# A fused four-layer network on one core: the scan layer's dt projected tile by tile, its output projection and its state sums moved in the engines' order

## The chip, the cores and the metric

The kernel runs on one core of a Trainium2 chip. A core has five engines with queues of their own: TensorE (PE, with its weight loads shown apart as PEld), VectorE (DVE), ScalarE (ACT), GpSimd (POOL) and SyncE (SP, which here only issues DMAs). Each works through its own queue in order, and they wait for each other through semaphores. The metric is device time in microseconds, the median of the runs. The kernel before takes 3452.4 us (three runs, 3451.87 to 3458.52). The profile is one more execution of the same program.

## The reference

Four residual layers follow each other, each on the group-normalised image `x` of shape (3, 256, 48, 48): an attention block, a 3x3 convolution whose kernel is mixed from 8 experts, a plain 3x3 convolution, and a selective scan (Mamba). The change is in the scan layer alone. Cut to what matters it computes, for each image, over 2304 tokens in order:

```python
xn = layernorm(x) * norm_w + norm_b              # 256 channels per token
x_in, z = split(in_proj(xn))                     # 512 each
u = silu(causal_conv4(x_in) + conv_b)
dt_raw, B, C = split(x_proj(u))                  # 16, 16, 16
dt = softplus(dt_proj(dt_raw) + dt_proj_b)       # 512
h = h * exp(dt * A) + dt * B * u                 # 512 x 16 states, per token
y = (sum over states of h * C + u * D) * silu(z)
out = out_proj(y)                                # 256, added to x
```

## The kernel before

The first three layers end at about 2020 us of the span; the rest is the scan layer. Tokens go in chunks of 384 (`CH`), 18 chunks in all, 6 for each image. The 512 inner channels are 4 tiles of 128 (`m`). For the scan itself 32 channels times 4 states lie on the 128 partitions, so a tile needs 16 scans of 384 tokens.

A chunk is 8 **steps** (`m`, `h`): four tiles in two halves of 8 scans each. One scan (`scan`, L1766, on DVE) reads a decay `exp(dt * A)` from one of three slots `ps_da`, which ACT fills (`decay`, L1758): decay number n + 3 is issued behind scan n, so ACT works three scans ahead and no more. The driving term `dt * u * B` is filled into `hs` half by DVE (`fill_upper`, L1719, from PSUM) and half by POOL (L1733). After a step POOL multiplies the states by C (`times_c`, L1783), and a step later PE sums them over the states into `ps_y` (`add_states`, L1795 and L1800). `spread_pe` (L1689) spreads half of the dt * u rows over the partitions for DVE's fill, `spread` (L1681) does the other half and dt itself by DMA from DRAM, where `keep_dt` has put them (L1335, L1337). `gate` (L1807, DVE) multiplies the sum by silu(z), three steps behind.

All other work of the layer is laid between the scans by hand. A step has two **half-steps** of four scans, so a chunk has 16, numbered j = 0 to 15. Each has places at which stages are issued: MID (behind the second scan and its decay), DONE (behind the third), LATE (behind the fourth) and PE_ (in even half-steps behind LATE; in odd ones at the end of the step, behind `fill` and `times_c`, and ahead of `add_states` and `spread_pe`). Three lists say which stage goes where, and for which chunk: `plan` prepares the next chunk (+1) and the norm of the one after (+2), `after` finishes z and writes the output of the previous chunk (-1), `gating` projects z. `keep_order` ties PE, DVE, ACT and POOL to the written order within the scans. SP's queue is not tied: the planner that builds the program places the DMAs by its own costs, so their order is seen only in the trace. The conv layers ahead of the scans, among whose products `early_preparation` lays the first chunk's stages, are ordered by the planner too.

Two PSUM banks (`bank[0]`, `bank[1]`, shown as ps_g) serve all these stages, so a stage's matmul waits until the copy of the stage before has emptied its bank. The stages which the change touches, by line: `group_scale` L1213, `less_mean` L1222, `square_mean` L1229, `centre` L1235 and L1237, `inverse_root` L1241 and L1242, `normalise` L1246, `taps` (conv and u projection) L1264, `take_u` L1273, `silu` L1278 with the return to the exp and ln tables at L228, `project_u` L1284, `take_dbc` L1292, `project_dt` L1310, `softplus` L1319 to L1321, `take_dt` L1326 and L1327, `keep_dt` L1331, `project_z` L1341, `take_z` L1349, `project_y` L1353 and L1355, `store` L1365.

## Time and profile before

| | us |
|---|---|
| median of three runs | 3452.4 |
| the profiled execution | 3452.73 |
| its span, first to last instruction | 3451.2 |
| first scan starts | 2025.81 |
| last scan starts | 3428.7 |
| one chunk in the middle (2721.98 to 2800.41) | 78.43 |
| POOL busy in it | 76.33 |
| DVE busy in it | 75.43 |
| PE busy in it | 66.34 |
| ACT busy in it | 61.62 |

A line of the timeline gives the start, the length in us, the engine, the line of the kernel, the operation with its output and inputs, and how many of a kind were merged; in brackets stands how long the engine had been idle before, and what ended that. In a view of waits, a line names who waited for whom, the total in us, how often, and the longest. In a view of stretches, busy times by engine are followed by the clock granted to PE, the DMA share and GB/s. The names `x`, `u`, `wconv` stand for big buffers that the scan layer reuses: for instance `ps_g L1310 out of wconv` is the projection of dt. The scan period repeats with a chunk; the chunk whose half-step 0 starts at 2734.23 is the one most often looked at.

### The profile page before, as it was taken

What the parts mean: (1) busy time and instruction counts of PE and PEld (TensorE: products, weight loads), DVE (VectorE), ACT (ScalarE), POOL (GpSimd) and SP (SyncE); (2) the same over time, 40 slices, a digit from 0 to 9 for tenths busy, and PEclk for the clock granted to TensorE, in tenths of its full rate; (3) what the DMA queues carried; (4) which work ended last, traced back from release to release, by engine and by line L of the source; (5) the groups of instructions that cost most, each with busy time, mean ns of one, the idle gap of its engine ahead of it and who ended that gap; (6) DMA issues with size and microseconds to landing.
All of it is one profiled execution on the core that took longest, in us unless ns stands there. A gap on an engine that the chain in (4) does not pass through costs nothing. (4 is left out here: it accounts for less than half of the span.)

```text
span 3451.2 us, 51999 instructions
## 1 busy us (share of the span) xinstructions
PE 3115.5 (90%) x20170; PEld 1496.8 (43%) x20170; DVE 2937.4 (85%) x3306; ACT 2353.3 (68%) x3508; POOL 1430.3 (41%) x385
## 2 busy tenths in 40 slices
PE   7999999999999999879999988888888888888885
PEld 4334343443433335457677753333344443333331
DVE  4799899859899994589965379999999999999998
ACT  3788888748888884422224467777777777777774
POOL 0000000000000001110000059999999999999997
PEclk9999999999999999999999998889999999988987
DMA  4000000010000003756302134444544444544441
GB/s 178 14 8 10 8 10 8 8 42 5 11 6 8 10 8 112 240 190 222 133 22 67 46 97 115 109 105 114 120 102 115 102 109 113 119 114 107 116 111 43
DMA packets 167603, 273.95 MB, mean 79 GB/s; under 512 B 30049, under 2 KB 134561, under 8 KB 165426
## 3 DMA queue, kind: packets, MB, share of 16 engines
q1 hardware_dynamic: 154114, 250.48, 26.9%
q10 hardware_dynamic: 13232, 20.06, 1.8%
q8 instruction: 160, 2.62, 0.3%
q14 instruction: 97, 0.79, 0.1%
HBM read 223.12 MB, written 47.10 MB: 78 GB/s over the span
## 5 line engine op out<-in xcount | busy, mean ns | idle before, releaser
L641 ACT ACTIVATE pt<-ps_s 128x1024 f32<-128x1024 f32 x972 | 942.4, 1022 | 154.7 <-PE ps_s L637 142.1
L1766 DVE TENSOR_TENSOR_SCAN hs<-ps_da,hs 128x385 f32<-128x385 f32 x1152 | 1003.9, 937 | 30.7 <-ACT ps_da L1758 27.3
L856 DVE TENSOR_TENSOR part<-part,pt 128x2048 f32<-128x2048 f32 x396 | 906.7, 2290 | 41.2 <-ACT pt L641 18.4
L1758 ACT ACTIVATE ps_da<-dtr,u 128x384 f32<-128x384 f32 x1152 | 656.5, 583 | 244.1 <-DVE hs L1766 225.9
L163 POOL TENSOR_TENSOR rstd<-ve,mhalf 128x2 f32<-128x2 f32 (+1 forms) x26 | 16.4, 631 | 1475.9 <-DVE ve L161 1475.9
L637 PE MATMUL ps_s<-q,kt 32*128 32x512 f32 (+1 forms) x4320 | 576.4, 592 | 0.1
L650 PE MATMUL acc<-pt,vt 128*32 128x512 f32 (+1 forms) x4320 | 520.9, 561 | 0.2
L1783 POOL TENSOR_TENSOR hc<-hs,x 128x3072 f32<-128x3072 f32 x72 | 445.6, 6188 | 18.9 <-DVE hs L1766 16.0
L1513 PE MATMUL ps_c<-vt,u 128*128 128x288 f32 x1728 | 432.7, 411 | 20.5 <-DVE u L262 20.5
L1783 POOL TENSOR_TENSOR hc<-hs,bc 128x3072 f32<-128x3072 f32 x71 | 437.8, 6166 | 17.3 <-DVE hs L1766 15.1
L1264 PE MATMUL ps_g<-u 128*128 128x384 f32 x1152 | 388.6, 492 | 7.4 <-ACT sz L1349 3.2
L1513 PEld LDWEIGHTS ps_c<-vt,u 128*128 128x128 f32 x1728 | 330.7, 192 | 117.1 <-issue 18.8
L1264 PEld LDWEIGHTS ps_g<-u 128*128 128x128 f32 x1152 | 214.8, 190 | 180.3 <-ACT ps_da L1758 19.3
L637 PEld LDWEIGHTS ps_s<-q,kt 32*128 32x128 f32 x4320 | 195.2, 183 | 199.1 <-issue 120.2
L1800 PE MATMUL ps_y<-hc,u 128*32 128x384 f32 x2304 | 245.0, 548 | 19.6 <-POOL hc L1783 19.1
L1733 POOL TENSOR_TENSOR hs<-dtur,x 128x1536 f32<-128x1536 f32 x72 | 248.9, 3457 | 6.3 <-DMA dtur<-dtud 6.3
L1733 POOL TENSOR_TENSOR hs<-dtur,bc 128x1536 f32<-128x1536 f32 x72 | 248.5, 3451 | 0.0
L650 PEld LDWEIGHTS acc<-pt,vt 128*32 128x32 f32 x4320 | 94.4, 108 | 353.4 <-issue 326.7
L1310 PE MATMUL ps_g<-wconv,u 17*128 17x384 f32 x144 | 79.2, 684 | 85.0 <-ACT x L1331 85.0
L1800 PEld LDWEIGHTS ps_y<-hc,u 128*32 128x32 f32 x2304 | 64.2, 117 | 177.8 <-issue 143.1
L1222 PE MATMUL ps_g<-wconv,u 128*128 128x384 f32 x144 | 80.3, 725 | 62.1 <-ACT x L1331 62.1
L321 POOL MEMSET xpad<- 128x212 f32 x12 | 5.7, 472 | 313.4 <-ACT xpad L1564 234.9
(246 smaller groups left out, 3624.0 us busy)
## 6 DMA issues: line engine op xcount, KB each, us to landing
wconv<-in_we SPq DMA_DIRECT2D x144, 384.0 KB, 4.2
dtr<-dtd SPq DMA_DIRECT2D x288, 192.0 KB, 3.9
dtur<-dtud SPq DMA_DIRECT2D x288, 96.0 KB, 4.2
wconv<-xd SPq DMA_DIRECT2D x36, 384.0 KB, 4.3
x<-bcd SPq DMA_DIRECT2D x72, 192.0 KB, 6.0
dtd<-x SPq DMA_DIRECT2D x36, 384.0 KB, 3.1
bc<-bcd SPq DMA_DIRECT2D x72, 192.0 KB, 6.0
yc<-ycat ACTq DMA_DIRECT2D x18, 576.0 KB, 4.7
```

Of the source, the lines that this page charges most:

```text
L637: nc.tensor.matmul(s[:, j, cols], kt[r, mt * P : (mt + 1) * P], q[r, :n], start=True, stop=True,)
L641: nc.scalar.activation(p[:, h0 : h0 + 2, :], s, AF.Exp)
L650: nc.tensor.matmul(acc[h * HD : (h + 1) * HD, :n], vt[:, mt, g * P + h * HD : g * P + (h + 1) * HD], p[:, h, cols], start=mt == 0, stop=mt ...
L856: ): nc.vector.tensor_tensor(part, first, p, ALU.add)
L1222: nc.tensor.matmul(bank[to], w3v["less"][:, int(to != ct), :], k.xg[:, ct, :], start=ct == 0, stop=ct == CT - 1,)
L1264: nc.tensor.matmul(bank[m % 2], w3v["wtap"][:, tap, ct, m * P : (m + 1) * P], k.xn[:, ct, tap : tap + CH], start=tap == 0 and ct == 0, sto ...
L1513: nc.tensor.matmul(pc[:, :HN], u[:, i, dy, ct, m * P : (m + 1) * P], vt[:, i, ct, dy * TW : dy * TW + HN], start=ct == 0 and dy == 0, stop ...
L1733: nc.gpsimd.tensor_tensor(states(s)[:, :, 2:4, 1:], chunks[at].rows[m][1].unsqueeze(1).broadcast_to([P, 2, 2, CH]), b_rows(s, 0, 2), ALU.mult,
L1758: nc.scalar.activation(slots[n % 3][:, 1 : CH + 1], chunks[at].rows[m][0][:, q, :], AF.Exp, scale=amat[:, col : col + 1],)
L1766: nc.vector.tensor_tensor_scan(b, slots[(8 * s + part) % 3][:, : CH + 1], b, 0.0, ALU.mult, ALU.add)
L1783: nc.gpsimd.tensor_tensor(hc, tiles[s][:, :, :, 1:], cb.broadcast_to([P, 2, 4, CH]), ALU.mult)
L1800: nc.tensor.matmul(k.y_ps[32 * q : 32 * q + 32, :CH], fold, hc[:, g, q, :], start=False, stop=h == 1 and g == 1,)
```

## The change

Everything is in the scan layer.

- dt goes tile by tile (m = 0 to 3) instead of in two pairs, through bank 0: `project_dt`, `softplus`, `take_dt` and `keep_dt` each work on one tile and have places of their own from half-step 8 to 14. Softplus has three operations of 384 columns per tile; before, Abs was done per tile, and Exp and Ln once for the 768 columns of a pair. `keep_dt` writes its two DRAM tensors per tile, 8 DMAs per chunk instead of 4, and `spread` reads from these.
- There is a new place BEGIN, behind the first scan and decay of a half-step.
- The output projection of the previous chunk goes through bank 1 in both halves. The first is issued in half-step 6 (before: 5) and stored in 8 (6), so it stands ahead of the product of u with the x projection (`project_u`, half-step 7); the second is issued at BEGIN of 9, behind the projection of the first dt tile (before: 6, ahead of `project_u`), and stored in 10 (8).
- At the end of a step, `add_states` and `spread_pe` are issued ahead of the stages of PE_ and no longer behind them. Among these stages are, in half-step 1, 3 and 7, the product of u's tile 1 (`taps`), of tile 2, and `project_u`; in 13 and 15 the squared mean and z.
- The norm of the chunk after next is centred in two pieces through bank 1 into a tile of its own, `xc`; the squares go into `xg`, and `normalise` reads `xc`. Its stages are moved by up to one half-step, as is the first of z.
- The tile `dtur` loses its 16 padding columns.

```diff
--- before.py
+++ after.py
@@ -1135,7 +1135,7 @@
         rooms["xn"] = [w3v["xn0"], w3v["xn1"]]
         pieces = [wst.tile([P, 3 * 256], F32, name="wconv") for _ in range(6)]
         halves = [t.rearrange("p (t n) -> p t n", t=2) for t in pieces]
-        for name, got in zip(("xg", "sq", "ot"), (halves[:2], halves[2:3], halves[3:5])):
+        for name, got in zip(("xg", "xc", "ot"), (halves[:2], halves[2:3], halves[3:5])):
             rooms[name] = got
         rooms["dbc"] = [halves[5][:96, j, :] for j in range(2)]
 
@@ -1215,26 +1215,27 @@
                 bias=sh[:, ct : ct + 1], scale=sc[:, ct : ct + 1],
             )
 
-    def less_mean(k):
-
-        for to in range(CT):
-            for ct in range(CT):
-                nc.tensor.matmul(
-                    bank[to], w3v["less"][:, int(to != ct), :], k.xg[:, ct, :],
-                    start=ct == 0, stop=ct == CT - 1,
-                )
+    def less_mean(k, to, at=1):
+
+        for ct in range(CT):
+            nc.tensor.matmul(
+                bank[at], w3v["less"][:, int(to != ct), :], k.xg[:, ct, :],
+                start=ct == 0, stop=ct == CT - 1,
+            )
+
+    def centre(k, to, at=1):
+        if to == 0:
+            k.xc = room(k, "xc")
+        nc.scalar.copy(k.xc[:, to, :], bank[at])
+
+    def squares(k):
+        nc.scalar.activation(k.xg, k.xc, AF.Square)
 
     def square_mean(k):
         for ct in range(CT):
             nc.tensor.matmul(
-                bank[1], mean2, k.sq[:, ct, :], start=ct == 0, stop=ct == CT - 1
+                bank[1], mean2, k.xg[:, ct, :], start=ct == 0, stop=ct == CT - 1
             )
-
-    def centre(k):
-        for ct in range(CT):
-            nc.scalar.copy(k.xg[:, ct, :], bank[ct])
-        k.sq = room(k, "sq")
-        nc.scalar.activation(k.sq, k.xg, AF.Square)
 
     def inverse_root(k):
         var = bank[1]
@@ -1243,7 +1244,7 @@
 
     def normalise(k):
         rs = bank[1].unsqueeze(1).broadcast_to([P, CT, CH])
-        nc.vector.tensor_tensor(k.xg, k.xg, rs, ALU.mult)
+        nc.vector.tensor_tensor(k.xg, k.xc, rs, ALU.mult)
 
     def tokens(k):
 
@@ -1304,37 +1305,32 @@
         k.dt = room(k, "dt")
         k.dtu = room(k, "dtu")
 
-    def project_dt(k, m0):
-        for j in range(2):
-            m = m0 + j
-            nc.tensor.matmul(
-                bank[j], w3v["dtsb"][:, m * P : (m + 1) * P], k.dbc[: DTR + 1, :],
-                start=True, stop=True,
-            )
-
-    def softplus(k, m0):
-
-        both = k.dt[:, m0 : m0 + 2, :]
-        for j in range(2):
-            nc.scalar.activation(k.dt[:, m0 + j, :], bank[j], AF.Abs)
-        nc.scalar.activation(both, both, AF.Exp, scale=-1.0)
-        nc.scalar.activation(both, both, AF.Ln, bias=1.0)
-
-    def take_dt(k, m0):
-        for j in range(2):
-            m, pdt = m0 + j, bank[j]
-            nc.vector.scalar_tensor_tensor(pdt, pdt, 0.0, k.dt[:, m, :], ALU.max, ALU.add)
-            nc.vector.tensor_tensor(k.dtu[:, m, :], pdt, k.u[:, m, :], ALU.mult)
-
-    def keep_dt(k, m0):
-        for j in range(2):
-            nc.scalar.copy(k.dt[:, m0 + j, :], bank[j])
-        if m0 == 0:
+    def project_dt(k, m, at=0):
+        nc.tensor.matmul(
+            bank[at], w3v["dtsb"][:, m * P : (m + 1) * P], k.dbc[: DTR + 1, :],
+            start=True, stop=True,
+        )
+
+    def softplus(k, m, at=0):
+
+        t = k.dt[:, m, :]
+        nc.scalar.activation(t, bank[at], AF.Abs)
+        nc.scalar.activation(t, t, AF.Exp, scale=-1.0)
+        nc.scalar.activation(t, t, AF.Ln, bias=1.0)
+
+    def take_dt(k, m, at=0):
+        p = bank[at]
+        nc.vector.scalar_tensor_tensor(p, p, 0.0, k.dt[:, m, :], ALU.max, ALU.add)
+        nc.vector.tensor_tensor(k.dtu[:, m, :], p, k.u[:, m, :], ALU.mult)
+
+    def keep_dt(k, m, at=0):
+        nc.scalar.copy(k.dt[:, m, :], bank[at])
+        if m == 0:
             k.dtd, k.dtud = {}, {}
-        d = k.dtd[m0] = dram.tile([P, 2, CH], F32, name=f"dtd{m0}")
-        nc.sync.dma_start(d, k.dt[:, m0 : m0 + 2, :])
-        d = k.dtud[m0] = dram.tile([P // 2, 2, CH], F32, name=f"dtud{m0}")
-        nc.sync.dma_start(d, k.dtu[P // 2 :, m0 : m0 + 2, :])
+        d = k.dtd[m] = dram.tile([P, CH], F32, name=f"dtd{m}")
+        nc.sync.dma_start(d, k.dt[:, m, :])
+        d = k.dtud[m] = dram.tile([P // 2, CH], F32, name=f"dtud{m}")
+        nc.sync.dma_start(d, k.dtu[P // 2 :, m, :])
 
     def project_z(k, m, j):
         for ct in range(CT):
@@ -1348,12 +1344,12 @@
             k.sz = room(k, "sz")
         nc.scalar.copy(k.sz[:, m, :], bank[j])
 
-    def project_y(k, mo, lo=0, hi=DI):
+    def project_y(k, mo, lo=0, hi=DI, at=1):
         if lo == 0:
-            nc.tensor.matmul(bank[mo], ident, k.ot[:, mo, :], start=True, stop=False)
+            nc.tensor.matmul(bank[at], ident, k.ot[:, mo, :], start=True, stop=False)
         for m in range(lo, hi):
             nc.tensor.matmul(
-                bank[mo], w("out", m * 256 + mo * P, P), k.sz[:, m, :],
+                bank[at], w("out", m * 256 + mo * P, P), k.sz[:, m, :],
                 start=False, stop=m == DI - 1,
             )
 
@@ -1361,21 +1357,24 @@
         k.ot = room(k, "ot")
         nc.sync.dma_start(k.ot, xd[k.b][:, :, k.c * CH : (k.c + 1) * CH])
 
-    def store(k, mo):
-        nc.scalar.copy(k.ot[:, mo, :], bank[mo])
+    def store(k, mo, at=1):
+        nc.scalar.copy(k.ot[:, mo, :], bank[at])
         nc.sync.dma_start(
             out[k.b, mo * P : (mo + 1) * P, k.c * CH : (k.c + 1) * CH], k.ot[:, mo, :]
         )
 
 
 
-    MID, DONE, LATE, PE_ = range(4)
+    BEGIN, MID, DONE, LATE, PE_ = range(5)
     plan = [
-        (12, MID, 2, group_scale),
-        (12, PE_, 2, less_mean),
-        (13, LATE, 2, centre),
+        (11, BEGIN, 2, group_scale),
+        (11, PE_, 2, lambda k: less_mean(k, 0)),
+        (12, MID, 2, lambda k: centre(k, 0)),
+        (12, PE_, 2, lambda k: less_mean(k, 1)),
+        (13, DONE, 2, lambda k: centre(k, 1)),
+        (13, LATE, 2, squares),
         (13, PE_, 2, square_mean),
-        (14, MID, 2, inverse_root),
+        (14, DONE, 2, inverse_root),
         (15, MID, 2, normalise),
         (15, LATE, 2, tokens),
         (0, PE_, 1, lambda k: taps(k, 0, 0, 4)),
@@ -1390,13 +1389,21 @@
         (7, PE_, 1, project_u),
         (8, LATE, 1, take_dbc),
         (8, PE_, 1, lambda k: project_dt(k, 0)),
-        (9, LATE, 1, lambda k: softplus(k, 0)),
-        (10, MID, 1, lambda k: take_dt(k, 0)),
-        (10, DONE, 1, lambda k: keep_dt(k, 0)),
-        (10, PE_, 1, lambda k: project_dt(k, 2)),
-        (11, LATE, 1, lambda k: softplus(k, 2)),
-        (12, MID, 1, lambda k: take_dt(k, 2)),
-        (12, DONE, 1, lambda k: keep_dt(k, 2)),
+        (9, MID, 1, lambda k: softplus(k, 0)),
+        (9, LATE, 1, lambda k: take_dt(k, 0)),
+        (10, BEGIN, 1, lambda k: keep_dt(k, 0)),
+        (10, BEGIN, 1, lambda k: project_dt(k, 1)),
+        (10, DONE, 1, lambda k: softplus(k, 1)),
+        (11, MID, 1, lambda k: take_dt(k, 1)),
+        (11, DONE, 1, lambda k: keep_dt(k, 1)),
+        (11, DONE, 1, lambda k: project_dt(k, 2)),
+        (12, BEGIN, 1, lambda k: softplus(k, 2)),
+        (12, DONE, 1, lambda k: take_dt(k, 2)),
+        (12, LATE, 1, lambda k: keep_dt(k, 2)),
+        (12, LATE, 1, lambda k: project_dt(k, 3)),
+        (13, MID, 1, lambda k: softplus(k, 3)),
+        (13, LATE, 1, lambda k: take_dt(k, 3)),
+        (14, BEGIN, 1, lambda k: keep_dt(k, 3)),
     ]
 
     after = [
@@ -1404,15 +1411,15 @@
         (0, MID, 0, lambda k: k.at and take_z(k, 3, 1)),
         (3, LATE, 0, lambda k: silu(k.sz)),
         (2, MID, -1, residual),
-        (5, PE_, -1, lambda k: project_y(k, 0)),
-        (6, LATE, -1, lambda k: store(k, 0)),
-        (6, PE_, -1, lambda k: project_y(k, 1)),
-        (8, MID, -1, lambda k: store(k, 1)),
+        (6, PE_, -1, lambda k: project_y(k, 0)),
+        (8, MID, -1, lambda k: store(k, 0)),
+        (9, BEGIN, -1, lambda k: project_y(k, 1)),
+        (10, MID, -1, lambda k: store(k, 1)),
     ]
 
     gating = [
-        (13, PE_, 1, lambda k: project_z(k, 0, 0)),
-        (14, DONE, 1, lambda k: take_z(k, 0, 0)),
+        (14, BEGIN, 1, lambda k: project_z(k, 0, 0)),
+        (14, LATE, 1, lambda k: take_z(k, 0, 0)),
         (14, PE_, 1, lambda k: project_z(k, 1, 0)),
         (15, MID, 1, lambda k: take_z(k, 1, 0)),
         (15, PE_, 1, lambda k: project_z(k, 2, 0)),
@@ -1439,9 +1446,11 @@
         yield
         for tap in (0, 1):
             fold_taps(winx, cwb, tap)
-        less_mean(k)
+            less_mean(k, tap, tap)
         yield
-        centre(k)
+        for ct in range(CT):
+            centre(k, ct, ct)
+        squares(k)
         yield
         square_mean(k)
         yield
@@ -1467,7 +1476,16 @@
         nc.scalar.activation(k.u, k.u, AF.Silu)
         yield
         k = chunks[1]
-        for stage in (group_scale, less_mean, centre, square_mean, inverse_root, normalise):
+        group_scale(k)
+        yield
+        for ct in range(CT):
+            less_mean(k, ct, ct)
+        yield
+        for ct in range(CT):
+            centre(k, ct, ct)
+        squares(k)
+        yield
+        for stage in (square_mean, inverse_root, normalise):
             stage(k)
             yield
         tokens(k)
@@ -1482,15 +1500,11 @@
         yield
         take_dbc(k)
         yield
-        for m in (0, 2):
-            project_dt(k, m)
-            yield
-            softplus(k, m)
-            yield
-            take_dt(k, m)
-            yield
-            keep_dt(k, m)
-            yield
+        for m0 in (0, 2):
+            for stage in (project_dt, softplus, take_dt, keep_dt):
+                for j in range(2):
+                    stage(k, m0 + j, j)
+                yield
         for m in (0, 2):
             for j in range(2):
                 project_z(k, m + j, j)
@@ -1673,9 +1687,9 @@
         def spread(k, m):
 
             dtr = scn.tile([P, 4, CH], F32, name="dtr")
-            dtur = scn.tile([P, 2, 16 + CH], F32, name="dtur")[:, :, 8 : 8 + CH]
+            dtur = scn.tile([P, 2, CH], F32, name="dtur")
             for t, src in ((dtr, k.dtd), (dtur, k.dtud)):
-                src = src[m & 2][:, m & 1, :]
+                src = src[m]
                 for i in range(4):
                     r = slice(32 * i, 32 * i + 32)
                     nc.sync.dma_start(t[r], src.rearrange("(q d) n -> d q n", d=32))
@@ -1829,6 +1843,8 @@
                         chunks[c].rows = {**rows, n: spread(chunks[c], n)}
                 if part == 4 and s + 1 < len(steps):
                     first_states(s + 1)
+                if part % 4 == 0:
+                    run(at, j, BEGIN)
                 if part % 4 == 1:
                     run(at, j, MID)
                 if part % 4 == 2:
@@ -1843,23 +1859,22 @@
                 fill(s + 1)
             last_states(s)
             times_c(s)
-            run(at, 4 * m + 2 * h + 1, PE_)
             if s >= 1:
                 add_states(s - 1)
-
             if h == 0 and s + 2 < len(steps):
                 spread_pe(chunks[steps[s + 2][0]], steps[s + 2][1])
+            run(at, 4 * m + 2 * h + 1, PE_)
 
         end = len(steps) - 1
         k = chunks[last]
         residual(k)
         for mo in range(2):
-            project_y(k, mo, 0, DI - 1)
+            project_y(k, mo, 0, DI - 1, mo)
         add_states(end)
         gate(*steps[end][:2])
         for mo in range(2):
-            project_y(k, mo, DI - 1, DI)
-            store(k, mo)
+            project_y(k, mo, DI - 1, DI, mo)
+            store(k, mo, mo)
         keep_order(tc, listed, mark)
     late_pools.close()
 
```

## The prediction

> **What bounds the kernel now.** The page comes first, for which stage the change touches.
>
> ```profile
> PE 3115.5 (90%) x20170; PEld 1496.8 (43%) x20170; DVE 2937.4 (85%) x3306; ACT 2353.3 (68%) x3508; POOL 1430.3 (41%) x385
> ...
> DVE  4799899859899994589965379999999999999998
> ...
> POOL 0000000000000001110000059999999999999997
> ```
>
> PE leads over the whole span, but the scan layer is the part from slice 23 on, where DVE and POOL are both full. Its first scan starts at 2025.81 and the chunks follow each other evenly, so one chunk is read closely. Three of them, cut where POOL waits:
>
> ```profile
> 2721.98:2800.41 78.43, 66.34 (x281) 30.70 (x280) 75.43 (x90) 61.62 (x120) 76.33 (x16) 0.89 0.47 112
> 2800.41:2878.98 78.57, 66.49 (x282) 30.88 (x281) 75.47 (x90) 61.63 (x120) 76.52 (x16) 0.91 0.46 112
> 2878.98:2957.45 78.47, 66.32 (x282) 30.72 (x281) 75.41 (x90) 60.85 (x113) 76.40 (x17) 0.91 0.46 112
> ```
>
> The columns are length, then busy PE, PEld, DVE, ACT, POOL. A chunk takes 78.4 us; POOL has 76.4 us of work in it and DVE 75.1 (by starts: 8 steps of 6.83, four fills of 0.85 and four of 2.53, four gates of 0.45, twice 2.14 for dt, 0.84 for the normalisation). Who waits for whom is read from POOL's timeline, and for ten chunks from the waits.
>
> ```profile
> 2716.77 3.49 POOL L1733 TENSOR_TENSOR hs<-dtur,x 128x1536 f32<-128x1536 f32 x1
> 2721.98 6.17 POOL L1783 TENSOR_TENSOR hc<-hs,x 128x3072 f32<-128x3072 f32 x1 [1.73 <-DVE hs L1766]
> 2728.11 3.44 POOL L1733 TENSOR_TENSOR hs<-dtur,bc 128x1536 f32<-128x1536 f32 x1
> ```
>
> ```profile
> ACT wconv L1365 <- PE ps_g L1355: 16.7, 10, 1.7
> DVE hs L1766 <- ACT ps_da L1758: 14.9, 19, 0.9
> DVE ps_g L1326 <- ACT x L1321: 6.3, 10, 0.6
> ```
>
> POOL stands still once a chunk for DVE, and DVE never waits for POOL until 3407. So DVE sets the pace: 75.1 of work and 3.3 of waits. A wait that DVE loses or gains moves the chunk one for one, until all of them come below 76.4 - 75.1 = 1.3 us, where POOL takes over. The four waits, by the start of a DVE instruction against the start without a wait: 0.82 in half-step 7 (the eighth scan at 2767.02, due 2766.20: ACT's store copy waits 1.67 for the output projection and the decay behind it is late); 0.71 in half-step 10 (dt taken at 2702.55, due 2701.84: softplus not ready); 0.96 in half-step 14 (scan at 2727.81, due 2726.85: behind centring, squares and inverse root on ACT); 0.85 at the end of half-step 3 (gate and fill, below). Sum 3.34, and 75.1 + 3.3 = 78.4.
>
> ```profile
> 2737.11 10.59 PE L1264 MATMUL ps_g<-u 128*128 128x384 f32 x32 [0.38 <-ACT sz L1349]
> ...
> 2747.63 1.50 PE L1800 MATMUL ps_y<-hc,u 128*32 128x384 f32 x16
> 2747.74 0.58 ACT L1273 ACTIVATE x<-ps_g,vec 128x384 f32<-128x384 f32 x1
> ...
> 2748.22 1.20 ACT L1758 ACTIVATE ps_da<-dtr,u 128x384 f32<-128x384 f32 x2
> ...
> 2749.06 0.91 PE L1689 MATMUL ps_r<-dtu,u 32*128 32x384 f32 x4
> 2749.19 0.56 DVE L1807 TENSOR_TENSOR x<-ps_y,x 128x384 f32<-128x384 f32 x1 [0.40 <-PE ps_y L1800]
> 2749.43 1.28 ACT L1278 ACT_TABLE_LOAD   x1
> ...
> 2750.02 2.62 DVE L1719 TENSOR_TENSOR hs<-ps_r,bc 128x1536 f32<-128x1536 f32 x2 [0.27 <-PE ps_r L1689]
> ```
>
> The two conv products of u (tiles 0 and 1, 16 instructions each) run in one piece to 2747.70. ACT is free at 2747.71 and takes tile 1 of u at once: there is no slack. The sums over states and the spread of dtu start only then, so DVE's gate is 0.47 late and its fill another 0.38.
>
> **Part by part.** Times t run from a step's first scan; scan k starts at 0.854k. The decay for scan k+3 can start at 0.98 + 0.854k, takes 0.55 to 0.58, and so has 1.0 us to spare; ACT makes up 0.3 a scan. What ACT is given beyond that, DVE waits for.
>
> *Sums and spread ahead of the products of odd half-steps.* The gate and fill of half-step 3 find their results ready: -0.85. But tile 1's product now waits behind 1.43 (the sums, 2747.63 to 2749.06) and 0.84 (the spread, to 2749.90). It ends at 2749.97, and ACT takes u 2.27 later; queued behind it are two decays, the silu of z with two table loads, then the decay for scan 3. That last one ends today at 2754.21; of the 2.27 about 0.1 was idle, so it ends at 2756.38. The step's first scan comes 0.85 earlier, at 2751.70, so scan 3 is due at 2754.26: a wait of 2.15. Net +1.30, in the 16 chunks that have a previous one and a next one. Bounds: 0 if PE gets ahead by 2.2, 2.5 if the moved pieces run at the rate of 2711.97 (2.79 for 16 against 1.50). I take 2.15, since PE is busy without a break there and its row is the warm one.
>
> *Output projection.* The first half goes to half-step 6 with its store in 8, the second to the start of 9 with its store in 10; each has some 4 us more before ACT asks, against 1.67 missing: -0.82, for 16 chunks (the last is POOL's: DVE waits for POOL there).
>
> *dt by tiles.* Softplus becomes three operations of 384 per tile. The nearest rows: Exp of 384 takes 475 ns (L1242), Abs 476 (L1319), so 1.49 with the gaps; bounds 1.3 (pairs back to back, 0.42 each) and 1.7 (Ln with a bias tile, 0.56 each). DVE's eight operations keep their 4.28.
> - Tile 0: softplus behind the decay of t = 5.41 to 5.96 (2697.86 in the step of 2692.45), so Ln ends at 7.45; DVE wants it after its last scan, 6.83: 0.65. Its matmul can start when dbc is taken (4.92) and is done by 5.9.
> - Tile 1, half-step 10: decay to 1.56, keep copy 2.0, decay 2.55, store copy 3.0, decay 3.5, softplus 5.0, decay 5.55; scan 6 is due at 5.12: 0.45. Taking dt itself waits for nothing.
> - Tile 2, half-step 12: softplus 1.54 to 3.03; DVE takes it after three scans, 2.56: 0.47.
> - Tile 3, half-step 13: again a decay and 1.49 in the time of two scans, 0.46, and its product waits for tile 2's copy, up to 0.3 more: 0.58.
>
> Sum 2.15 for 0.71 today: +1.44 in 17 chunks. Half-step 12's take is no longer a burst of two, but DVE's total is the same, so that is worth nothing while DVE has no lead over POOL.
>
> *Norm of the chunk after next.* Centring in two pieces, squares at the end of 13, the inverse root at "done" of 14. In my walk the tightest decays end at 4.83 (due 5.12) and 5.80 (due 5.98), with z's copy moved behind them: -0.96 in 16 chunks; from -0.96 to -0.6.
>
> *Nothing.* Four more small DMAs a chunk, at 0.34 and 0.49 each on SP, 1.7 us: SP stands for ACT most of the time (144.6 us for the keep copies alone in ten chunks). The next chunk's dt rows leave SP behind tile 2's copy as today (t = 6.64 then, about 6.5 now). If that cover goes, a rival below. The rows of dtur lose their 16 padding columns; no row prices that, I take 0 (POOL's 3.45 has 3 us of room a chunk).
>
> *Ahead of the scans.* There the tables are not preloaded, and Exp and Ln load one at each change; two per pair of tiles now becomes four.
>
> ```profile
> 1999.72 1.28 ACT L1321 ACT_TABLE_LOAD   x1
> ...
> 2007.21 2.75 PE L1341 MATMUL ps_g<-u 128*128 128x384 f32 x8
> ```
>
> Each load is 1.28, the next operation starts 0.01 to 0.02 behind it. Pair one ends 2.6 later and leaves 2.3 of it to pair two, which adds 2.9: the keep copies end near 2009.6, and the z product of 2007.21, with the last conv products behind it, waits 2.4. I take +2.4; from 0 (another order there) to 5.2 (four loads in full). [...]
>
> Sum: 16 x 1.30 = 20.8; -16 x 0.82 = -13.1; 17 x 1.44 = 24.5; -16 x 0.96 = -15.4; +2.4: **+19.2 us**. Span 3451.2, its execution 3452.73, 0.3 above the median of 3452.4; so 3471.6.
>
> **Rivals.**
> 1. Tile 1's product is in time after all (PE ahead in half-step 1): the wait of 2.15 is gone, -34.4: 3437, faster. It decides from a wait below 0.95 (19.2 / 16 less than 2.15). For it: PE is busy 66 of 78 us. Against: the products cannot start before z's tiles are copied (0.38 waited at 2737.11).
> 2. Softplus costs DVE nothing in tiles 0, 2 and 3 (ACT a scan ahead, or operations at 0.42): -1.7 x 17 = -28.9: 3443. Against: each sits two scans before its use.
> 3. PE cold before half-step 0. Sums, then z's last two tiles, follow pauses of 1.5 us; at 2706.72 four instructions took 2.92 after 5.05 idle, against 1.55. Then z is copied 1.3 late and tile 1 of u 0.85: +2.15 x 16: 3506. Against: after a pause of 1.44 (2724.63) they were fast.
> 4. The next chunk's dt rows leave SP behind tile 3's copy, at t near 2 of step 14: they land about 6 us later than now, POOL's fill slips and DVE waits some 1.9 for it: +32: 3504. SP's order is the planner's, not the written one.
> 5. Waits trade places and it ends within 0.2%.
>
> **How the numbers follow.** Mine 0.50 (its own range, with 0.2 on each of four softplus waits, 0.35 on three other places and the prologue's bounds: 3455 to 3490); rivals 1 and 2 0.13 and 0.10; 3 and 4 0.09 each; 5 0.09. About 0.2%, 7 us, is what can be told from no change: faster 0.23, same 0.11 (rival 5 and my low edge), slower 0.66. For 8 in 10 the range has to take in part of both sides: 3437 to 3501.
>
> **What would show it.** ACT's take of u at half-step 3 waiting about 2.3 for PE; scan 3 of half-step 4 waiting 2.1 for ACT; no wait of the store copies; DVE waits of 0.4 to 0.7 before three of the four dt takes; the chunk at 79.4. Wrong if the chunk is below 78.4, if that u copy waits for nothing, or if POOL waits for a DMA each chunk.

## The result and the profile after

The changed kernel takes 3514.1 us, median of four runs (3511.68 to 3517.93); the kernel before, run beside it, 3452.5. The ratio is 1.0175, 95% interval 1.0158 to 1.0193: slower by 61.6 us, where 19.2 were forecast. The sign was right; the time lies above the range.

The profiled execution took 3517.93 and has a span of 3515.9. Its first scan starts at 2031.73 (before: 2025.81), so 58.8 of the 65.2 us between the two profiled executions lie in the scan layer (1484.2 us against 1425.4). The first scan's start is a poor measure of the work ahead of it: in the fourteen profiles of this study it lies between 2022.4 and 2032.7, also among kernels in which nothing ahead of the scans differs. Line numbers after the change differ from those before: scan L1780, decay L1772, the take of dt L1323, the copy that keeps it L1327, less_mean L1221, centring L1229, the take of u L1274.

The busy line of the page:

```profile
PE 3170.2 (90%) x20170; PEld 1503.6 (43%) x20170; DVE 2937.9 (84%) x3306; ACT 2360.4 (67%) x3582; POOL 1432.3 (41%) x385
```

DVE and POOL have the work they had: 0.5 and 2.0 us more. PE takes 54.7 us more for the same 20170 instructions, ACT 7.1 more for 74 instructions more. For DVE and POOL, then, the loss is waiting. Two chunks, cut where POOL waits (columns: length, then busy PE, PEld, DVE, ACT, POOL, and after these the clock granted to PE):

```profile
2675.65:2757.59 81.94, 69.23 (x282) 30.83 (x281) 75.48 (x89) 61.81 (x124) 76.51 (x16) 0.90 0.45 107
2757.59:2839.55 81.96, 69.21 (x282) 30.87 (x281) 75.47 (x89) 61.84 (x124) 76.49 (x17) 0.90 0.45 107
```

A chunk takes 81.96 where it took 78.43. DVE still has 75.1 to 75.5 of work in it and POOL 76.5. POOL's timeline shows who is late: it waits for DVE several times a chunk, about 3.1 at the longest.

```profile
2757.59 6.20 POOL L1797 TENSOR_TENSOR hc<-hs,x 128x3072 f32<-128x3072 f32 x1 [3.07 <-DVE hs L1780]
```

Whom DVE waits for is in the view of waits, here over ten chunks (us in total, how often, the longest):

```profile
POOL hc L1797 <- DVE hs L1780: 45.9, 37, 3.1
DVE hs L1780 <- ACT ps_da L1772: 32.0, 19, 2.3
DVE ps_g L1323 <- ACT x L1319: 31.3, 41, 1.1
ACT wconv L1229 <- PE ps_g L1221: 30.2, 19, 2.6
```

Two of the old waits are gone: that of the store copy for the output projection (16.7 in the same view before), and those of gate and fill at the end of half-step 3. In their place scans wait for decays, the four takes of dt wait for softplus, and ACT's centring waits for PE: 30.2 in these ten chunks, where the same view of before has 2.6. The first of these places, as forecast, is the product of u's tile 1. ACT stands in front of it, and the decay for scan 3 stands behind that:

```profile
2705.03 0.58 ACT L1274 ACTIVATE u<-ps_g,vec 128x384 f32<-128x384 f32 x1 [2.49 <-PE ps_g L1265]
...
2711.42 4.36 DVE L1780 TENSOR_TENSOR_SCAN hs<-ps_da,hs 128x385 f32<-128x385 f32 x5 [2.26 <-ACT ps_da L1772]
```

The second was not forecast. From half-step 9 to 13 of the same chunk PE's timeline reads, with the copy and the scan that stand at its end:

```profile
2733.34 3.99 PE L1351 MATMUL ps_g<-sz,u 128*128 128x384 f32 x8
2737.26 1.50 PE L1814 MATMUL ps_y<-hc,u 128*32 128x384 f32 x16
...
2745.62 1.64 PE L1309 MATMUL ps_g<-wconv,u 17*128 17x384 f32 x2 [5.38 <-ACT x L1327]
2747.19 1.65 PE L1809 MATMUL ps_y<-x,diag 128*128 128x384 f32 x2
2748.77 2.79 PE L1814 MATMUL ps_y<-hc,u 128*32 128x384 f32 x16
2751.49 2.24 PE L1221 MATMUL ps_g<-wconv,u 128*128 128x384 f32 x4
...
2753.77 0.48 ACT L1229 COPY wconv<-ps_g 128x384 f32<-128x384 f32 x1 [2.54 <-PE ps_g L1221]
...
2754.77 2.66 DVE L1780 TENSOR_TENSOR_SCAN hs<-ps_da,hs 128x385 f32<-128x385 f32 x3 [1.10 <-ACT ps_da L1772]
```

After a pause of 5.38, in which it waits for the copy of dt tile 1, PE runs at about half its pace: the sums take 2.79 for 16 instructions, against 1.50 eleven microseconds earlier. Since the change the sums stand *ahead* of less_mean, so all of their slow 2.79 lies in front of ACT's centring, and behind that are the decays.

The waits of DVE in a chunk, by the start of an instruction against its start without a wait, beside the forecast:

| place | forecast | measured |
|---|---|---|
| scan 3 of half-step 4 (u's tile 1) | 2.15 | 2.35 |
| dt tile 0 / 1 / 2 / 3 | 0.65 / 0.45 / 0.47 / 0.58 | 0.71 / 0.97 / 0.55 / 1.11 |
| the scan behind the first centring, half-step 12 | 0 | 1.20 |
| store of the output; gate and fill of half-step 3 | 0 | 0 |
| sum | 4.30 | 6.89 |

75.1 + 6.89 = 81.99, which is the chunk of 81.96 to within 0.03.

### The profile page after: what moved, and what is told of

Its sections match the earlier page's. It is cut to its first block, busy times and chain, and to the rows that moved or that the text cites. A ratio compares the mean times of both kernels' runs of the same rounds, so it can differ in the third digit from the quotient of the medians.

```text
span 3515.9 us, 52262 instructions
## 1 busy us (share of the span) xinstructions
PE 3170.2 (90%) x20170; PEld 1503.6 (43%) x20170; DVE 2937.9 (84%) x3306; ACT 2360.4 (67%) x3582; POOL 1432.3 (41%) x385
## 5 line engine op out<-in xcount | busy, mean ns | idle before, releaser
L1780 DVE TENSOR_TENSOR_SCAN hs<-ps_da,hs 128x385 f32<-128x385 f32 x1152 | 1002.2, 935 | 60.4 <-ACT ps_da L1772 58.3
L1772 ACT ACTIVATE ps_da<-dtr,u 128x384 f32<-128x384 f32 x1152 | 657.1, 580 | 239.4 <-DVE hs L1780 219.3
L1309 PE MATMUL ps_g<-wconv,u 17*128 17x384 f32 x144 | 79.1, 636 | 151.8 <-ACT x L1327 126.2
L1733 DVE TENSOR_TENSOR hs<-ps_r,x 128x768 f32<-128x768 f32 (+1 forms) x108 | 127.9, 1210 | 2.2 <-DMA xd<-vt 2.1
```

Source lines behind the costliest of these rows:

```text
L1733: nc.vector.tensor_tensor(states(s)[:, lo:hi, 0:2, 1:], k.ps[:, :, :CH].unsqueeze(1).broadcast_to([P, hi - lo, 2, CH]), b_rows(s, lo, hi), ...
L1772: nc.scalar.activation(slots[n % 3][:, 1 : CH + 1], chunks[at].rows[m][0][:, q, :], AF.Exp, scale=amat[:, col : col + 1],)
L1780: nc.vector.tensor_tensor_scan(b, slots[(8 * s + part) % 3][:, : CH + 1], b, 0.0, ALU.mult, ALU.add)
```

## The experiments

Twelve kernels ran. "Chunk" is the mean of the last 14 periods from one chunk's normalisation to the next, in the profile; "before" is the time of the kernel before on the same chip. after, c3, a5 and a7 are medians of 4 to 10 runs; each other new kernel ran once, as did the kernel before beside a1, a2, a3 and b1. Over all chips the kernel before lies between 3447.6 and 3458.5, so differences of a few us between single runs say nothing.

| kernel | us | before | chunk |
|---|---|---|---|
| before | 3452.5 | | 78.5 |
| after | 3514.1 | 3452.5 | 81.96 |
| a1_sums_back | 3464.4 | 3450.7 | 79.29 |
| a2_tap1_first | 3480.0 | 3450.7 | 80.21 |
| a3_warm | 3487.4 | 3450.7 | 80.20 |
| b1_sums_ahead | 3533.8 | 3450.7 | 83.38 |
| c1_store_later | 3449.5 | 3456.2 | 78.52 |
| c2_three_places | 3443.4 | 3456.2 | 77.80 |
| c3_four_places | 3441.3 | 3456.2 | 77.80 |
| a4_take_u1_later | 3456.7 | 3456.2 | 78.61 |
| a5_takes_later | 3449.6 | 3454.3 | 78.15 |
| a6_dt_takes_only | 3489.5 | 3454.3 | 80.46 |
| a7_later_and_warm | 3416.8 | 3453.0 | 76.37 |
| a8_later_one_warm | 3433.4 | 3453.0 | 77.30 |

### Is it the place of the sums?

**a1_sums_back** is the changed kernel with the stages of PE_ in odd half-steps back ahead of the sums, as in the kernel before.

```diff
             times_c(s)
+            run(at, 4 * m + 2 * h + 1, PE_)
             if s >= 1:
                 add_states(s - 1)
             if h == 0 and s + 2 < len(steps):
                 spread_pe(...)
-            run(at, 4 * m + 2 * h + 1, PE_)
```

> The changed kernel with one part undone: at the end of a step the stages of the odd half-steps stand ahead of the sums over states again. Theory (order and a cold PE): the chunk of 81.95 us loses the wait of 2.35 at scan 3 of half-step 4, gets back 0.85 at the gate and fill of half-step 3, and, since less_mean no longer stands behind 2.7 us of slow sums, loses the 1.20 at centring and about 0.5 before tile 3 of dt: chunk near 78.8, time near 3459 (3451 to 3470). Rival (dt by tiles alone costs the time, the sums are harmless): chunk stays above 81, time above 3495.

3464.4; chunk 79.29. So 49.6 of the 61.6 us go with this one line, and the rest of the change, all together, costs about 14. The chunks are not alike, though: they take 78.2, 79.8 or 81.2. What differs between them is PE, for instance at the product of u with the x projection:

```profile
2692.30 4.51 PE L1285 MATMUL ps_g<-u 128*96 128x384 f32 x8 [2.13 <-ACT u L1279]
```

The same eight instructions take 2.82 in a good chunk. Here PE loses time after an idle time of only 2.13.

**a2_tap1_first** leaves the sums ahead, save in half-step 1, where the product of u's tile 1 goes first.

```diff
+            if 4 * m + 2 * h == 0:
+                run(at, 1, PE_)
             if s >= 1:
                 add_states(s - 1)
             ...
-            run(at, 4 * m + 2 * h + 1, PE_)
+            if 4 * m + 2 * h != 0:
+                run(at, 4 * m + 2 * h + 1, PE_)
```

> The changed kernel, but in half-step 1 alone the product of u's tile 1 stands ahead of the sums over states; elsewhere the sums stay ahead. Theory: only the wait at scan 3 of half-step 4 goes (2.35) and 0.85 returns at the gate and the fill of half-step 3; chunk 80.45, time 3490 (3484 to 3496). Rival (POOL or SP would take the place): chunk at least 81.5. Rival (that product sets everything): chunk 78.5 or less.

3480.0; chunk 80.21, alternating between 79.8 and 80.6. The wait of 2.35 at scan 3 goes; the gate's 0.40 and the fill's 0.27 come back, as before the change. That wait is worth about 34 us of the loss when it is traded for gate and fill; the time lies 4 us below the forecast of 3484 to 3496.

**b1_sums_ahead** makes the same move in the kernel *before*, and nothing else.

```diff
             times_c(s)
-            run(at, 4 * m + 2 * h + 1, PE_)
             if s >= 1:
                 add_states(s - 1)
-
             if h == 0 and s + 2 < len(steps):
                 spread_pe(...)
+            run(at, 4 * m + 2 * h + 1, PE_)
```

> The kernel before with one part of the change alone: sums and spread ahead of the stages of odd half-steps. Theory: ACT's take of u's tile 1 waits 2.3, scan 3 of half-step 4 waits 2.2, the 0.85 at half-step 3 goes, and the squared mean stands behind sums and spread, so the wait of half-step 14 grows by about 0.85: chunk 78.43 + 1.35 + 0.85 = 80.6, time near 3487 (3475 to 3495). Rival (the sums ahead are harmless without the other parts): chunk 78.6 or less, time within 5 us of before.

A miss by 47 us: 3533.8, chunk 83.38. The scans wait 2.33 behind u's tile 1, as expected, but also 1.73 behind the store (its projection now stands behind the sums as well; the copy's wait grows from 1.67 to 2.66), 1.57 to 1.93 at half-step 14, and 1.03 to 1.06 in half-step 0. The last of these is a forecast that was made for the changed kernel and did not come true there, PE slow ahead of half-step 0 (rival 3):

```profile
2770.61 0.91 PE L1795 MATMUL ps_y<-x,diag 128*128 128x384 f32 x2 [2.04 <-DVE x L1807]
2771.45 2.51 PE L1800 MATMUL ps_y<-hc,u 128*32 128x384 f32 x16
2773.89 3.48 PE L1341 MATMUL ps_g<-u 128*128 128x384 f32 x8
```

So the move alone costs 83 us, and the other parts of the change, which cost 14 without it, take 20 back with it: the later output projection has taken one of these waits away. The parts don't add up; a term for each of them by itself was not a sound sum.

### Is it PE's pace?

**a3_warm** leaves all of the change and puts 14 instructions of PE, products that nothing reads, into the pause of half-step 10.

```diff
+    def warm(k):
+        for _ in range(7):
+            nc.tensor.matmul(
+                bank[1], w("out", 0, P), k.u[:, 0, :], start=True, stop=True
+            )
 ...
     plan = [
+        (10, LATE, 1, warm),
```

> The changed kernel with 7 products (14 matmul instructions, some 4.6 us) more per chunk in half-step 10, written to bank 1 and overwritten by less_mean, so that PE has no pause of 5.4 us before dt's tile 2. Results are the same. Theory (the pause makes PE slow for the next 8 us): the projection of tile 2, the sums and less_mean together fall from 8.1 us to about 4, centring waits for nothing, tile 3's wait falls from 1.11 to 0.55: chunk 80.2, time near 3486 (3478 to 3494). Rival (less_mean is late because it is queued behind the sums, at whatever speed, or the extra products only delay PE): centring still waits 2 or more, chunk 81.9 or more, time 3512 or more.

3487.4, chunk 80.20: 26.7 us gained by adding work. PE's timeline over the same stages as above:

```profile
2725.61 4.78 PE L1358 MATMUL ps_g<-u 128*128 128x384 f32 x14
2731.06 0.91 PE L1309 MATMUL ps_g<-wconv,u 17*128 17x384 f32 x2 [0.67 <-ACT x L1327]
...
2732.74 1.50 PE L1821 MATMUL ps_y<-hc,u 128*32 128x384 f32 x16
2734.17 1.56 PE L1221 MATMUL ps_g<-wconv,u 128*128 128x384 f32 x4
2739.33 1.64 PE L1309 MATMUL ps_g<-wconv,u 17*128 17x384 f32 x2 [3.61 <-ACT x L1327]
2740.91 2.93 PE L1221 MATMUL ps_g<-wconv,u 128*128 128x384 f32 x4
```

The sums take 1.50 and not 2.79, less_mean 1.56 and not 2.24, and the first centring waits no more: the 1.20 is PE's pace, shown by filling the pause and changing nothing else. The next pause, of 3.61, is followed by slow rows again, one stage later.

The same run settles tile 1 of dt, for its chunks alternate. Where the output projection ahead of that tile runs at full pace, the take waits for nothing; where it does not, the take waits 0.89 in the bracket, which is 0.97 by its start, as in the changed kernel.

```profile
2638.58 2.74 PE L1351 MATMUL ps_g<-x,u 128*128 128x384 f32 x8
2646.62 0.54 DVE L1323 SCALAR_TENSOR_TENSOR ps_g<-ps_g,x 128x384 f32<-128x384 f32 x1
...
2718.33 4.44 PE L1351 MATMUL ps_g<-sz,u 128*128 128x384 f32 x8
2727.35 0.57 DVE L1323 SCALAR_TENSOR_TENSOR ps_g<-ps_g,x 128x384 f32<-128x384 f32 x1 [0.89 <-ACT x L1319]
```

The traces also record the clock granted to PE, and the slow rows can be laid beside it. In the changed kernel, cut into equal stretches between the places where the clock changes (length, PE's busy time and instructions, clock, DMA share, GB/s):

```profile
2729.01:2732.42 3.41, 1.84 (x6) 1.00 0.19 65
2732.42:2735.84 3.42, 3.42 (x6) 0.50 0.03 7
...
2739.25:2742.66 3.41, 0.99 (x6) 1.00 0.89 210
2742.66:2746.08 3.42, 0.46 (x1) 0.50 1.01 208
2746.08:2749.49 3.41, 3.41 (x12) 0.50 1.09 296
2749.49:2752.90 3.41, 3.41 (x18) 0.50 1.09 216
2752.90:2756.32 3.42, 1.46 (x5) 1.00 0.26 56
2756.32:2759.73 3.41, 3.41 (x9) 0.50 0.28 87
```

Every slow row shown above for the changed kernel overlaps a stretch at 0.50. The clock is at 0.50 there for 3.41 us at a time or for three times that (10.24, from 2742.66 to 2752.90). A chunk's clock is 0.90 after the change and 0.89 to 0.91 before it: what changed is which products stand at half clock, and who waits for them.

The pauses of 5.38 and 3.61 here were followed by rows that took 1.4 to 1.9 times as long. A shorter one was followed by slow rows too: in a1_sums_back, behind 2.13, the eight products with the x projection took 4.51 instead of 2.82. And PE had not stood still through the stretches of 3.41 ahead of half clock in the fence above: they still held 1.84, 0.99 and 1.46 us of its work. So a pause of 2 us is not safe in these traces.

### Does the loss hang on the one take of u?

**a4_take_u1_later** changes one digit of the changed kernel: ACT's take of u's tile 1 comes a half-step later, in 4.

```diff
-        (3, MID, 1, lambda k: take_u(k, 1)),
+        (4, MID, 1, lambda k: take_u(k, 1)),
```

> The changed kernel, with tile 1 of u taken behind the second scan of half-step 4 instead of 3, nothing else. Theory: the sums ahead of its product cost only because ACT asks for it too early; the wait of 2.35 at scan 3 of half-step 4 goes, the gate stays in time: chunk 79.6, time near 3476 (3470 to 3482). Rival (PE as such is too late there, and the next products hand it on): chunk 81 or more, time above 3498.

3456.7, where 3476 was expected (3470 to 3482): this one place is worth 57 us, nearly the whole loss, and the kernel is then as fast as the one before (3456.2 beside it). The chunk falls by 3.35 where the wait at scan 3 is 2.35. Most of the rest is the wait at the centring, which costs DVE nothing here: PE recovers sooner from the same pause.

```profile
2714.69 1.64 PE L1309 MATMUL ps_g<-wconv,u 17*128 17x384 f32 x2 [5.38 <-ACT x L1327]
...
2717.84 2.26 PE L1814 MATMUL ps_y<-hc,u 128*32 128x384 f32 x16
2720.03 1.56 PE L1221 MATMUL ps_g<-wconv,u 128*128 128x384 f32 x4
```

In the changed kernel the pause of 5.38 was followed by 2.79 and 2.24 for the same two stages. The takes of dt still wait 0.64, 0.89, 0.47 and 0.84 in this chunk; tile 1 waits in 8 of the 17 chunks and not at all in the others. The granted clock of this chunk is 0.93 in the mean (2654.64 to 2733.18), where the changed kernel has 0.90. Why PE recovers sooner here is not shown.

### Were the waits of the kernel before worth their length?

The forecast gave the output projection's move its full 0.82 a chunk. Three kernels, made from the kernel before, test such gains one by one. **c1_store_later** only moves the copy that stores the first output tile, so that it no longer waits.

```diff
-        (6, LATE, -1, lambda k: store(k, 0)),
+        (7, MID, -1, lambda k: store(k, 0)),
```

> The kernel before, with the first store of the output moved from half-step 6 to 7, nothing else: ACT no longer waits 1.67 for the output projection in the middle of a step. Theory (DVE sets the pace, a wait of DVE moves the chunk one for one): the 0.82 in half-step 7 goes and nothing takes its place; chunk 78.5 - 0.8 = 77.7, time 13 less, near 3438. Rival (POOL sets the pace, or the wait is handed on): chunk 78.3 or more, time within 4 us of before.

The rival was right: 3449.5, chunk 78.52, as before. The scan's wait of 0.82 is gone, but the gate and the fill that follow wait for PE:

```profile
2685.89 0.56 DVE L1807 TENSOR_TENSOR x<-ps_y,x 128x384 f32<-128x384 f32 x1 [0.36 <-PE ps_y L1800]
2686.72 2.62 DVE L1719 TENSOR_TENSOR hs<-ps_r,x 128x1536 f32<-128x1536 f32 x2 [0.27 <-PE ps_r L1689]
```

PE has no break there from the products of u in half-step 0 on. It is late for the whole stretch, and ACT's wait was only where this showed first.

**c2_three_places** adds two more: the take of the first dt pair, and the inverse root with the first z.

```diff
-        (14, MID, 2, inverse_root),
+        (14, DONE, 2, inverse_root),
...
-        (10, MID, 1, lambda k: take_dt(k, 0)),
-        (10, DONE, 1, lambda k: keep_dt(k, 0)),
+        (10, DONE, 1, lambda k: take_dt(k, 0)),
+        (10, LATE, 1, lambda k: keep_dt(k, 0)),
...
-        (14, DONE, 1, lambda k: take_z(k, 0, 0)),
+        (14, LATE, 1, lambda k: take_z(k, 0, 0)),
```

> The same with two more places changed: dt's first pair is taken one scan later (half-step 10, DONE, kept at LATE), and the inverse root of the norm and the copy of z's first tile one place later (DONE and LATE of half-step 14). Theory: 0.71 and some 0.7 of the 0.96 go as well, waits left near 1.1, which is below 1.3, so POOL takes over: chunk 76.5 to 76.9, time near 3424. Rival (the later places only hand the waits on): chunk above 77.3, time above 3432.

3443.4, chunk 77.80, and not 3424: of the 1.67 moved out of these two places 0.7 arrives. What remains are gates that wait 0.36 to 1.0 for PE, fills that wait 0.27 behind them, and in some chunks a scan that waits for its decay.

**c3_four_places** also lets the sums go first in half-step 1 alone, with the take of u later.

```diff
+            if 4 * m + 2 * h != 0:
+                run(at, 4 * m + 2 * h + 1, PE_)
             if s >= 1:
                 add_states(s - 1)
             ...
+            if 4 * m + 2 * h == 0:
+                run(at, 1, PE_)
...
-        (3, MID, 1, lambda k: take_u(k, 1)),
+        (4, MID, 1, lambda k: take_u(k, 1)),
```

> The same, and in half-step 1 alone the sums and the spread stand ahead of the product of u's tile 1, as in the change, while tile 1 of u is taken behind the second scan of half-step 4 instead of 3. Theory: the 0.85 at half-step 3 goes, and ACT doesn't meet the late product, as it asks 5 us later: waits left 0.2 to 0.4, but POOL is the floor at 76.4: chunk 76.4 to 76.6, time near 3421 (3415 to 3426), hardly less than with three places. Rival (the sums ahead cost, wherever u is taken): chunk above 77.5, time above 3435.

3441.3 (ratio to the kernel before 0.9956, 0.9942 to 0.9970), chunk 77.80, and not 3421. The gate of half-step 3 is in time, but the one of half-step 7 waits 0.94. The time is the one that the rival gave, but not for its reason: the chunk is as long as with three places, so the sums ahead neither cost nor gain here.

### The takes of dt

**a5_takes_later** is a4_take_u1_later with the takes of dt tiles 0, 2 and 3 one place later, and with them what follows; the take of tile 1 stays, though its projection moves.

```diff
-        (9, LATE, 1, lambda k: take_dt(k, 0)),
-        (10, BEGIN, 1, lambda k: keep_dt(k, 0)),
-        (10, BEGIN, 1, lambda k: project_dt(k, 1)),
+        (10, BEGIN, 1, lambda k: take_dt(k, 0)),
+        (10, MID, 1, lambda k: keep_dt(k, 0)),
+        (10, MID, 1, lambda k: project_dt(k, 1)),
...
-        (12, DONE, 1, lambda k: take_dt(k, 2)),
+        (12, LATE, 1, lambda k: take_dt(k, 2)),
...
-        (13, LATE, 1, lambda k: take_dt(k, 3)),
-        (14, BEGIN, 1, lambda k: keep_dt(k, 3)),
+        (14, BEGIN, 1, lambda k: take_dt(k, 3)),
+        (14, MID, 1, lambda k: keep_dt(k, 3)),
...
-        (14, BEGIN, 1, lambda k: project_z(k, 0, 0)),
+        (14, MID, 1, lambda k: project_z(k, 0, 0)),
```

> This kernel is the changed one with the first product of u taken in half-step 4 (as in a4) and the four takes of dt moved one or two places later on ScalarE, with the projections of dt that follow them. In a4 the scans still wait 0.64, 0.89, 0.47 and 0.84 us per chunk at those takes, 2.84 together. My theory: these waits are ScalarE's order alone; they go, and the chunk falls from 78.6 to between 76.4 and 77, where GpSimd's own work (76.4 to 76.5) sets the floor; the time is near 3423, up to 3432 if a product of TensorE comes late. The rival: TensorE, which restarts slowly after each of its pauses, takes the waits over, as it did when the store was moved in the kernel before; then the chunk stays at 78 or more and the time at 3447 or more.

3449.6 (ratio 0.9988, 0.9978 to 0.9997): a miss for the theory, though not in every chunk. The rival's slow restart "after each of its pauses" goes too far: behind 1.97 in a4_take_u1_later PE was at full pace (0.91 for the two of L1309). Two neighbours in the same profile, cut at the normalisation:

```profile
2651.43:2727.93 76.50, 65.07 (x281) 29.15 (x280) 75.19 (x90) 62.24 (x126) 75.94 (x17) 0.96 0.48 115
2727.93:2807.21 79.28, 68.61 (x280) 30.20 (x280) 75.43 (x90) 60.90 (x123) 78.45 (x17) 0.89 0.47 111
```

The first is at POOL's floor. The second has the same work and a lower granted clock, 0.89 against 0.96, and its timeline shows both the slow products and what DVE pays for them:

```profile
2786.97 1.64 PE L1309 MATMUL ps_g<-wconv,u 17*128 17x384 f32 x2 [5.38 <-ACT x L1327]
...
2790.12 2.79 PE L1814 MATMUL ps_y<-hc,u 128*32 128x384 f32 x16
...
2795.76 2.66 DVE L1780 TENSOR_TENSOR_SCAN hs<-ps_da,hs 128x385 f32<-128x385 f32 x3 [1.33 <-ACT ps_da L1772]
...
2807.21 0.95 DVE L1247 TENSOR_TENSOR wconv<-wconv,ps_g 128x768 f32<-128x768 f32 x1 [1.21 <-ACT ps_g L1243]
```

**a6_dt_takes_only** has the same moves, with the take of u left in half-step 3.

```diff
-        (4, MID, 1, lambda k: take_u(k, 1)),
+        (3, MID, 1, lambda k: take_u(k, 1)),
```

(against a5_takes_later)

> The changed kernel with the four takes of dt moved later as in a5, and the first product of u left where the change has it, in half-step 3. If the waits at dt and the wait at u are two separate losses, the waits at dt go (about 3 of the chunk's 6.9 us) and the 2.35 at u and the 1.2 at the centring stay: chunk near 79, time near 3466. If the wait at u sets TensorE's rhythm for the whole chunk, so that the later products come late whatever the order of the takes, the waits at dt stay at half or more and the time is at 3490 or above.

3489.5, chunk 80.46, at the edge of what the rival gave: in ten chunks 14.1 of the 31.3 at dt stay, and at the scans, where the changed kernel waits 32.0, it is 34.8. The centring waits 2.54 as in the changed kernel:

```profile
2739.28 0.48 ACT L1229 COPY wconv<-ps_g 128x384 f32<-128x384 f32 x1 [2.54 <-PE ps_g L1221]
```

### Is PE's pace all that is left?

**a7_later_and_warm** is a5_takes_later with products that nothing reads in two pauses, 14 instructions in half-step 10 and 8 in half-step 12; **a8_later_one_warm** has only the first.

```diff
+    def warm(k, n):
+        for _ in range(n):
+            nc.tensor.matmul(
+                bank[1], w("out", 0, P), k.u[:, 0, :], start=True, stop=True
+            )
 ...
     plan = [
+        (10, LATE, 1, lambda k: warm(k, 7)),
+        (12, DONE, 1, lambda k: warm(k, 4)),
```

> The kernel with the later takes (a5) and, in the two pauses of TensorE in which it waits for copies of dt, products that nothing reads: 14 instructions into bank 1 in half-step 10 and 8 in half-step 12, overwritten by the next use of the bank, so the results are the same. In a5 the chunks alternate between 76.5 us, which is GpSimd's work, and 78 to 79.3; in a chunk of 79.28 the scans wait 1.33 behind the first centring and 1.21 behind the inverse root, whose products ran slow behind a pause of 5.38. My theory: that slowness is all that is left, so every chunk comes to 76.4 to 77 and the time to 3423 to 3432. The rival: the alternation comes from something else (the order of the stages, a transfer), or the added work delays the real products as much as it helps; then the chunk stays at 77.8 or more, the time at 3444 or more.

> As a7, but only the 14 instructions in half-step 10. By my theory the wait behind the first centring goes and the one behind the inverse root may stay where the pause of 1.96 in half-step 12 slows TensorE again: chunks of 76.4 to 78, mean near 77.2, time near 3434. By the rival it stays like a5: mean 78.1, time near 3450.

3416.8 (3415.21 to 3421.24; ratio 0.9898, 0.9882 to 0.9915), below the 3423 to 3432 forecast, and 3433.4. Each filled pause gives about 16.5 us: 3449.6, 3433.4, 3416.8. Three chunks of a7_later_and_warm:

```profile
2629.77:2705.77 76.00, 70.20 (x302) 32.59 (x302) 75.06 (x91) 61.59 (x124) 76.00 (x17) 1.00 0.49 115
2705.77:2782.78 77.01, 71.63 (x302) 33.41 (x302) 75.07 (x91) 61.61 (x124) 77.01 (x18) 0.98 0.47 114
2782.78:2858.79 76.01, 70.20 (x302) 32.59 (x302) 75.06 (x91) 61.59 (x124) 75.89 (x16) 1.00 0.49 115
```

POOL is busy for 76.00 of 76.00 us, and the granted clock is 1.00 where it was 0.90 before and after the change. In the chunk of 77.01, with a clock of 0.98, one stage is still slow, the output projection ahead of dt's tile 1, and that tile's take waits for it:

```profile
2753.08 4.44 PE L1351 MATMUL ps_g<-x,u 128*128 128x384 f32 x8
...
2762.10 0.57 DVE L1323 SCALAR_TENSOR_TENSOR ps_g<-ps_g,x 128x384 f32<-128x384 f32 x1 [1.64 <-ACT x L1319]
```

In the next chunk the same stage takes 2.74 and the take comes 1.0 sooner. The wait costs nothing here: POOL works without a break through both chunks.

PE's busy time per chunk is 4 to 5 us above that before the change (66.3), the chunk is 2.1 shorter, and the scan layer takes 1391.1 us (3413.5 less a first scan at 2022.38) against 1425.4. This is the shortest time of the study, 36 us below the kernel before and 97 below the changed one.

## Why the prediction was right in sign and wrong in size

- **DVE sets the pace, with POOL's 76.4 as the floor.** Held. The chunk is DVE's work and its waits to within 0.03, and in a7_later_and_warm, where DVE's waits are down to 0.9 and 1.9 a chunk, the mean chunk of 76.37 is the floor that was named.
- **Sums and spread ahead, +1.30 a chunk.** Held: -0.85 and +2.35, so +1.50. ACT's take waits 2.49 for the forecast 2.27, scan 3 comes 2.35 late for 2.15. The place, the mechanism and the row (PE without a break, its fast row) were right. What the term left out is that the same move stands in half-steps 11 and 13 as well, where PE is slow: see the norm.
- **Output projection, -0.82.** The wait is gone as forecast. That it counts in full was an assumption: c1_store_later takes the same wait out of the kernel before and gains nothing a chunk, because gate and fill wait for PE in its place. In the changed kernel the sums stand ahead, so gate and fill are in time, and the chunk's sum of waits closes with the 0.82 in full; only there does it count.
- **dt by tiles, +1.44.** Mis-sized: +2.63 (3.34 less the old 0.71), 20 us over 17 chunks. Tiles 0 and 2 were right (0.71 and 0.55 for 0.65 and 0.47): they wait for softplus alone, and its three operations took what the rows said. Tiles 1 and 3 take 0.97 and 1.11 for 0.45 and 0.58. "Taking dt itself waits for nothing" was wrong for tile 1: that take waits, not scan 6. ACT asks for the product 1.11 before it is there, and PE has spent 3.99 on the output projection ahead of it, in part at a clock of 0.50 (to 2735.84), against 2.74 in good rows; where the projection is at full pace, in a1_sums_back and in every other chunk of a3_warm, the take waits for nothing. Tile 3 is not ACT's order alone: in a1_sums_back, with the same places on ACT and a centring that does not wait, it is 0.55 in nearly every chunk, close to the forecast. In a4_take_u1_later its product is at full pace (0.91), but the centring ahead of it waited 1.32 for PE, and from there ACT works without a gap; the take waits 0.84 in the bracket, where the changed kernel has 1.02. The walk priced both tiles as if PE were at full pace.
- **Norm, "from -0.96 to -0.6".** This step failed: +0.24. The old wait went, but a new one of 1.20 came at the first centring, behind sums at 2.79 and less_mean at 2.24. Over 16 chunks it is worth 19 us, and a3_warm shows its cause. The working had the row (16 sums in 2.79 at 2711.97) and used it as a bound in half-step 3, where PE never rests, and not in half-step 11, behind a pause of over 5 us that the trace of before shows in the same stretch of the chunk:

```profile
2706.72 2.92 PE L1310 MATMUL ps_g<-wconv,u 17*128 17x384 f32 x4 [5.05 <-ACT x L1331]
...
2711.97 2.79 PE L1800 MATMUL ps_y<-hc,u 128*32 128x384 f32 x16
```

- **The stretch ahead of the scans, +2.4.** Mis-sized: about 0.1 in the profiled pair. Of its 5.9, 5.8 stand already at 1939, where the two programs are alike, and are not the table loads'; their cause is open, and the stretch ends anywhere from 2022.4 to 2032.7 whatever the kernel. In the changed trace pair one has three loads of 1.28 where it had one, and pair two has two, as before.
- **SP and the added DMAs, nothing.** Held; the dt rows of the next chunk leave SP ahead of tile 2's copies, and rival 4 did not occur.

Put together, 16 x (1.50 - 0.82 + 0.24) + 17 x 2.63 = 59.4 against the 58.8 of the scan layer. Of the 42 us missed, 19 are the norm, which is PE's pace behind a pause, and 20 dt, nearly all of it at tiles 1 and 3: one behind a product that PE ran at half clock, one behind ACT, which PE's slow products had made late. Rival 3 named this mechanism and put it at half-step 0, where it did not show here (it did in b1_sums_ahead). Rivals 1 and 2 fell: tile 1 of u was not in time, and softplus did cost DVE.

What stays open: why, behind the same pause of 5.38, less_mean is back at 1.56 in a4_take_u1_later and takes 2.24 in the changed kernel; and what the other parts of the change cost one by one, since only their sum (14 us, a1_sums_back) was run.

## What to carry to other kernels

Before a stage is moved on PE's queue, look for the pauses ahead of its new place and price everything behind them by the slow rows of the trace, not the fast ones (here 2.79 for the sums, not 1.50); in a chain where ACT takes each product on the dot, half-pace PE passes straight into the pace of the whole (1.20 a chunk at the centring). A wait that is removed counts only if what comes next on that path has slack: move it alone first, and see whether it turns up at the next consumer. Where PE must pause, products that nothing reads can be worth tens of us (33 here, against 57 for the best single move), and a chain's strict copies should be asked for a place later than the product can be done.

## What the hardware showed that was not expected

- Work that nothing reads made the kernel faster: 22 instructions a chunk, 14 of which take 4.78 us in a3_warm, took 33 us off a kernel of 3450 (a5 to a7).
- A PE pause of 5.38 was followed by rows at 1.4 to 1.9 times their length for some 8 us in the changed kernel (2745.62 to 2753.7), and for 5 us in a4_take_u1_later. The pause of 1.97 that comes next was followed by full pace in a4_take_u1_later (0.91 for the two of L1309, 1.56 for the four of L1221) and by 1.07 and 2.93 for the same in the changed kernel. So the length of a pause alone did not decide.
- Chunks keep to a few lengths. The changed kernel gives 82.0 in nearly every chunk, a7_later_and_warm alternates between 76.0 and 77.0, a5_takes_later between several.
